# An encoder front's query and key buffer given back after the scores, with vector work placed between its matrix pieces

## The chip, the cores and the metric

The kernel runs on one core of a Trainium2 chip. The metric is the time of one execution in microseconds on the device. Five engines work side by side, each through its own instructions in order: TensorE (PE, with its weight loads shown apart as PEld), VectorE (DVE), ScalarE (ACT), GpSimd (POOL) and SyncE (SP). SP issues most transfers, POOL the gathers and scatters by index. An instruction that waits holds up everything behind it on its engine.

## What is computed

Two layers with residuals on x of shape (4, 1024, 256), in float32:

```python
x = x + attn(layernorm(x))     # causal attention, 16 heads of 16, slopes on the positions, over the 1024 tokens
x = x + ffn(layernorm(x))
# ffn, on its input z:
#   q, k, v = z @ in_proj_w.T     attention among the 4 batch entries of one token (4 x 4 scores, 16 heads)
#   h = layernorm(z + ctx @ out_w.T)
#   top two experts of 8 by h @ router_w.T; assign = the larger index of the two
#   out = layernorm(h + w2[assign](gelu(w1[assign](h))))
```

The second attention is small: for each token, the four batch entries look at each other. It needs no TensorE for scores and sums; VectorE multiplies and adds. The experts then need tokens sorted by expert, so they start from tables of which token goes where.

## The kernel before, in words

**Causal attention.** It is cut into 20 units: 12 of 256 queries (three chunks of four batch entries), then 8 of 128 queries. Each unit has four groups of heads, and each group some rounds. TensorE makes scores (tiles `sk`), ScalarE the exponentials (`p`), TensorE the weighted sums (`pv`). The rounds run in a fixed order, two per place: the loop at L2273 calls `score_next`, then `E_slot` (vector work), `D_slot` (matrix work of others), then `score_next`, `weigh_next` and `E_slot` again. So work of other parts enters TensorE's queue only at these places, between the two scores of a place.

**Encoder fronts.** `front(i, ...)` (L1573) does the second layer up to the router for block i, i = 0 to 7, 128 tokens of each of the four batch entries. It is a generator. At each yield it names the kind and the planned cost of its next piece: "E" and "P" vector work, "N" ScalarE, "R" a root on POOL, "D" matrix work, "d" matrix work that follows at once, "DQ" matrix work that needs the buffer `qkv`. The order in one front: statistics and norm into `u`; turn `u` into `ut` (D); add a bias row to x and store it (E); project to queries, keys, values and router columns, one batch entry t at a time (DQ, d, d, d); four score pieces, each a product `pr` and its sum over heads into `sc`; softmax of `sc`; four pieces of weighted values (`pv`, then sums into `ctx`); turn `ctx` (D); output projection `ao` added to `u` (D, d); norm, router key, the token's expert (`expert`, `hot`), its scaling and store; its place among the tokens of its expert (D). The last front (i = 7, `last=True`) makes the value half of the projection inside the score pieces and sums the weighted values on TensorE (`turned_sum`, L1694).

**The buffer.** Queries, keys, values and router columns of a front lie in one tile, `qkv`, 128 x 4 x 776 numbers, of which there is one. `held["qkv",]` is set when a front's DQ piece is issued (L2111 in the loop, L2366 in the tail) and removed at L1721, after the last weighted value. While it is set no other front issues its DQ. `pr` and `pv` share the tag "pr", with two buffers.

**Who comes when.** `running` holds at most two fronts; a front is queued when the last of its four units is added into x (`projected`, L2164) and starts when there is a place (`start_fronts`, L2070). `take_E` (L2076) goes over the running fronts and issues their vector pieces that are ready by the planner's own clock, as long as the planned VectorE is at most `AHEAD` = 1 us past the planned TensorE. `take_D` (L2100) issues matrix pieces up to a planned `D_SLOT` = 10 us per place, all pieces of one front as far as they go, then the other's; the planned costs are 2.8 for DQ and 2.6 for each d, so three of the four fit into one place. When front 5 is placed, `tabulate_first` (L1283) is put at the head of `running`: it makes the table of the tokens of blocks 0 to 5, 18 expert tiles of 128 tokens.

**The tail.** After the last weighted sum (L2290) what is left of the units is flushed: `invert`, `load_y`, `divide` (due_E) and `project` (due_D) of unit 18; the last unit is then normalised on TensorE and VectorE (`normalise(2)`, `normalise(3)`, L1135) and projected (`project_slots`, L1144), which completes x for front 7. Four calls of `experts.fetch` follow, each of which gathers a tile and loads its weights if a table is there; then `load_layer` loads the other weights. The loop at L2389 takes pieces of front 7, of whatever fronts still run, and of `prepare_rest`, by planned time, and puts steps of expert tiles (`tile_step`, L2381) where TensorE would be free before the next piece. It holds back the last 5 of the 18 tiles (`HELD_BACK`) until front 7's tokens are counted (`count_all`, L1257). `tabulate_rest` then makes the second table, and the other tiles run: 38 in all.

Of the kernel before, what the change touches and what calls it, by code (L numbers as in the profile page):

```python
# [29 lines left out]
F32 = mybir.dt.float32  # L30
# [3 lines left out]
ALU = mybir.AluOpType  # L34
# [3 lines left out]
P = 128  # L38
B, T, C = 4, 1024, 256
H, D, E = 16, 16, 8  # L40
S = 32
G = H // 4
NT = T // P
CC = C // P
QC = 512
# [560 lines left out]
def fast_layer(ctx: ExitStack, tc: tile.TileContext, odd, x, wq, wk, wv, wp, w_in, w_out, w_r,  # L606
# [26 lines left out]
    nc = Core(tc.nc, told)  # L633
# [92 lines left out]
    def wide(a):  # L726
        return a.unsqueeze(1).to_broadcast([P, B] + list(a.shape)[1:])
# [4 lines left out]
    at_row = con(Q_ROW)  # L732
    number_i = const("number_i", [P, 1], I32)
    nc.gpsimd.iota(number_i, pattern=[[0, 1]], base=0, channel_multiplier=1)
    pos = fact.tile([P, T], F32, tag="pr", name="pos", bufs=2)
    nc.gpsimd.iota(
        pos, pattern=[[1, T]], base=-T // 2, channel_multiplier=0,
        allow_small_or_imprecise_dtypes=True,
# [113 lines left out]
    held = {}  # L852
# [614 lines left out]
    def prepare_biases(stage):  # L1467

        if stage == 0:
            b1_rows = fact.tile([E, C], F32, tag="equal", name="b1_rows")
            nc.scalar.dma_start(
                b1_rows.rearrange("e (c p) -> e c p", p=P),
                b1.rearrange("p (e c) -> e c p", c=CC),
            )
            b2_rows = fact.tile([E, C], F32, tag="before", name="b2_rows")
            nc.scalar.dma_start(b2_rows, b2)
            b_row = fact.tile([1, 2 * C], F32, tag="u", name="b_row", bufs=2)
            for k, at in enumerate((B_IN, B_OUT)):  # L1480
                nc.scalar.dma_start(
                    b_row[:, k * C:(k + 1) * C], rows[at:at + C].unsqueeze(0)
                )
            held["biases"] = (
                (b1_rows, b_bf[0]), (b2_rows, b_bf[1]),
                (b_row[:, :C], in_bf), (b_row[:, C:], out_bf),
            )
            return
        src, three = held["biases"][stage - 1]
        if three is out_bf:  # L1490
            nc.vector.tensor_tensor(src, src, router["passed"][0:1, :C], ALU.add)
        n, width = src.shape
        rest = fact.tile([n, width], F32, tag="pr", name="rest", bufs=2)
        nc.vector.tensor_copy(rest, src)
        pieces = fact.tile([n, 3, width], BF16, tag="turned", name="pieces", bufs=TURNED)
        for k in range(3):
            nc.vector.tensor_copy(pieces[:, k], rest)
            nc.sync.dma_start(three[k * n:(k + 1) * n, :width], pieces[:, k])
            if k < 2:
                nc.vector.tensor_tensor(rest, rest, pieces[:, k], ALU.subtract)  # L1500
# [72 lines left out]
    def front(i, fact, more, last):  # L1573
# [43 lines left out]
            for_later(t)  # L1617
        store(("x", i), store_later)
        yield "DQ" if more else "D", 2.8
        qkv = fact.tile([P, B, 3 * C + E], F32, tag="qkv", name=f"qkv_{i}")  # L1620

        def projected_qkv(t, lo, hi):
            pq = bank(f"qkvp_{i}_{t}")[:, :hi - lo]
            for cc in range(CC):
                nc.tensor.matmul(
                    pq, ut[:, cc, t * P:(t + 1) * P], w_in_sb[:, cc, lo:hi],
                    start=cc == 0, stop=cc == CC - 1,
                )
                if not lo + cc:
                    nc.tensor.matmul(pq[:, :C], ones_bf, in_bf, start=False, stop=False)  # L1630
            if lo and not last:
                nc.vector.tensor_copy(qkv[:, t, lo:hi], pq)
            else:
                nc.scalar.copy(qkv[:, t, lo:hi], pq)

        for t in range(B):
            projected_qkv(t, 0, QC)
# [4 lines left out]

        def routed():
            nc.vector.tensor_tensor(
                u_[:, :, C:], qkv[:, :, 3 * C:], wide(router["b_out"]), ALU.add
            )

        if not last:
# [4 lines left out]
        for t in range(B):  # L1653
            yield "E", 2.4, 0.9 if last else 0.0
            if last:
                projected_qkv(t, QC, 3 * C + E)
            pr = fact.tile([P, B, C], F32, tag="pr", name=f"pr_{i}_{t}", bufs=2)
            nc.vector.tensor_tensor(pr, wide(qkv[:, t, 0:C]), qkv[:, :, C:2 * C], ALU.mult)
            nc.vector.tensor_reduce(
                sc[:, t], pr.rearrange("p s (h d) -> p s h d", d=D), AX.X, ALU.add  # L1660
            )
        yield "E", 1.1
        over_s = lambda a: a.rearrange("p t s h -> p t h s")
        top = small.tile([P, B, H], F32, tag="top", name=f"top_{i}", bufs=1)
# [11 lines left out]
        nc.vector.tensor_tensor(sc, sc, each_s(tot), ALU.mult)  # L1676

        def weighted(t):
            pr = fact.tile([P, B, C], F32, tag="pr", name=f"pv_{i}_{t}", bufs=2)
            nc.vector.tensor_tensor(  # L1680
                pr.rearrange("p s (h d) -> p s h d", d=D),
                qkv[:, :, 2 * C:3 * C].rearrange("p s (h d) -> p s h d", d=D),
                sc[:, t].unsqueeze(3).to_broadcast([P, B, H, D]),
                ALU.mult,
            )
            return pr
# [26 lines left out]
        else:  # L1713
            ctx_ = fact.tile([P, B, C], F32, tag="ctx", name=f"ctx_{i}")
            for t in range(B):
# [1 line left out]
                pr = weighted(t)  # L1717
                nc.vector.tensor_tensor(pr[:, 0:2], pr[:, 0:2], pr[:, 2:4], ALU.add)
                nc.vector.tensor_tensor(ctx_[:, t], pr[:, 0], pr[:, 1], ALU.add)
        if more:  # L1720
            held.pop(("qkv",))  # L1721
        if not last:
            if i < PC * (NC - 2):
                yield "N", 0
# [337 lines left out]
    def product(cost, what):  # L2062
        taken.clear()
        what()
        end = on_tensor(cost)
        busy("DVE", OF_D * cost, end - 0.5 * cost)
        read_at(max(end + READ, time["DVE"]))
        return end
# [7 lines left out]
    def take_E(some=True):  # L2076

        start_fronts()
        left = some
        while left:  # L2080
            left = False
            for it in list(running):
                now, kind = time["PE"], it.kind
                if kind not in ("E", "N", "R", "P"):
                    continue
                on = {"E": "DVE", "P": "DVE", "N": "ACT"}.get(kind)
                if it.ready > max(now, time[on] if on else 0.0) + EARLY_BY:
                    continue
                if on == "DVE" and time["DVE"] > now + AHEAD:
                    continue  # L2090
                if kind == "R":
                    it.ready = max(now, it.ready) + ROOT
                else:
                    it.ready = busy(on, it.cost if on == "DVE" else 0.5, it.ready)
                left = True
                it.next()
                if it.kind == "end":
                    running.remove(it)

    def take_D(cost):  # L2100

        for it in list(running):
            while it.kind[0] in "Dd":
                if it.kind == "DQ" and ("qkv",) in held:
                    break
                if it.kind != "d" and it.ready > time["PE"] + EARLY_BY:
                    break
                if cost and cost + it.cost > D_SLOT:
                    break
                if it.kind == "DQ":  # L2110
                    held["qkv",] = True  # L2111
                cost += it.cost
                end = product(it.cost, it.next)
                it.ready = max(end + READ, time["DVE"])
            if it.kind == "end":
                running.remove(it)

    begins = [0]
# [52 lines left out]
    def pop_due(due, now):  # L2171
        some = sorted((it for it in due if it[0] <= now), key=lambda it: it[0])
        for it in some:
            due.remove(it)
        return [(cost, what) for _, cost, what in some]
# [52 lines left out]
            experts.fetch()  # L2228
        take_E(some)

    def D_slot(p):
        todo = of_D.pop(p, []) + pop_due(due_D, time["PE"])
        for cost, what in todo:
            product(cost, what)
        take_D(sum(cost for cost, _ in todo))

    for p in range(-6, 0):
        E_slot(2 * p)
# [34 lines left out]
    for p in range(len(rounds) // 2):  # L2273
        then = p < len(rounds) // 2 - 1
        score_next(2 * p)
        E_slot(2 * p)
        D_slot(p)
        fill()
        take_E(then)
        score_next(2 * p + 1)  # L2280
        if len(waiting) > 2:
            weigh_next(waiting[:2])
            del waiting[:2]
        fill()
        E_slot(2 * p + 1, then)
# [5 lines left out]


    assert not of_E and not of_D, (sorted(of_E), sorted(of_D))
    for _, what in pop_due(due_E + [], 1e9) + pop_due(due_D + [], 1e9):
        what()
    for it in running:
        it.ready = 0.0
    for g in range(2, G):
        normalise(g)
    load_sums(last_unit)  # L2300
    project_slots()
    tail = ctx.enter_context(pool("tail", 1))
# [205 lines left out]
```

## Time and profile before

| what | us |
|---|---|
| time, median of 3 runs (lowest to highest) | 827.07 (824.54 to 828.95) |
| the profiled execution: its own time | 827.67 |
| the profiled execution: span of its instructions | 825.9 |
| busy: PE, PEld, DVE, ACT, POOL | 708.6, 532.4, 544.8, 416.5, 253.6 |
| last weighted sum of the causal attention begins | 617.66 |
| x complete for front 7 (`x<-x,op`) begins | 632.57 |
| first expert tile on PE (`mtp`) | 667.26 |
| `counts_all` of front 7's experts on PE | 723.86 |

All rows but the first are of one profiled execution. Times in the trace count from its span's start. Its own time is 1.8 us longer than its span. The program's helper for issuing is line 587, so most instructions carry L587 and have to be told apart by their tiles. A row of the time line reads: start, duration, engine, line, operation, out<-in, shape, count, and in brackets how long the engine had been idle and what ended that. One name can stand for a neighbour, since two products share a pair of PSUM banks: `qkv<-op` or `qkv<-qkp` is the copy of `qkvp` too.

### The profile page before, as it was taken

The numbers are of one execution on the slowest core, as the hardware profiler recorded it, in microseconds if no ns is written. First come the engines' busy times: TensorE is split into PE (matmuls) and PEld (weight loads), VectorE is DVE, ScalarE is ACT, GpSimd is POOL, SyncE is SP. The second block draws the span as 40 slices with busy tenths as digits, with TensorE's granted clock in tenths as the row PEclk, the third lists the DMA queues.
The fourth block names the chain that finished last, engine by engine and source line by source line (L and its number), as shares of the span: only waits on it lengthen the run. The fifth ranks groups of instructions, "written<-read, shape, count | busy, mean of one in ns | idle before, by whom it ended". The sixth has DMA issues, their size and how long they took to land. (4 is left out here: it accounts for less than half of the span.)

```text
span 825.9 us, 22497 instructions
## 1 busy us (share of the span) xinstructions
PE 708.6 (86%) x8917; PEld 532.4 (64%) x8917; DVE 544.8 (66%) x1316; ACT 416.5 (50%) x625; POOL 253.6 (31%) x360
## 2 busy tenths in 40 slices
PE   3988878999999999998998998999983689677882
PEld 2766656667666656565787876788662368566771
DVE  7335403739489768847966648497684779885663
ACT  1554535647547656635665757487550236233540
POOL 5533211313021222111222211122120235638885
PEclk9899898999999999999999999999995699988996
DMA  7444444435234234423554556255125512234430
GB/s 218 120 149 147 115 126 139 137 98 169 82 105 136 91 97 127 131 74 98 140 157 118 163 162 158 57 156 166 36 75 198 178 47 89 89 96 127 128 97 25
DMA packets 75220, 99.57 MB, mean 121 GB/s; under 512 B 19496, under 2 KB 58723, under 8 KB 74596
## 3 DMA queue, kind: packets, MB, share of 16 engines
q1 hardware_dynamic: 62272, 67.84, 28.3%
q10 hardware_dynamic: 7972, 16.05, 6.2%
q0 software_dynamic: 4864, 14.16, 5.7%
q8 instruction: 73, 1.20, 0.7%
q14 instruction: 39, 0.32, 0.1%
HBM read 61.55 MB, written 35.12 MB: 117 GB/s over the span
## 5 line engine op out<-in xcount | busy, mean ns | idle before, releaser
L587 ACT ACTIVATE p<-sk 128x1024 f32<-128x1024 f32 (+1 forms) x320 | 287.8, 939 | 160.6 <-PE sk L587 139.4
L1005 POOL TENSOR_SCALAR_AFFINE_SELECT p<-p 128x512 f32<-128x512 f32 (+1 forms) x160 | 105.6, 664 | 396.6 <-ACT p L587 394.6
L587 PE MATMUL sk<-slots 32*128 32x128 f32 (+1 forms) x3456 | 181.1, 328 | 21.5 <-DVE kq L587 8.4
L587 PEld LDWEIGHTS sk<-slots 32*128 32x128 f32 x3456 | 137.2, 187 | 65.0 <-issue 24.8
L587 PE MATMUL pv<-p,v 128*32 128x128 f32 (+1 forms) x3456 | 143.4, 312 | 9.9 <-DVE count L587 2.9
L587 PEld LDWEIGHTS pv<-p,v 128*32 128x32 f32 x3456 | 95.9, 110 | 46.9 <-issue 7.8
L587 PE MATMUL qkvp<-w_in,ut 128*128 128x264 f32 (+1 forms) x228 | 80.3, 488 | 0.0
L587 PEld LDWEIGHTS qkvp<-w_in,ut 128*128 128x128 f32 x228 | 40.8, 193 | 26.9 <-issue 22.4
L587 PE MATMUL oe<-w,ge 128*128 (+1 forms) x152 | 43.4, 410 | 14.4 <-DVE given L587 6.0
L587 PE MATMUL qkp<-xt,wqk 128*128 128x256 f32 x224 | 55.5, 392 | 0.2 <-ACT p L587 0.2
L1839 POOL DMA_INDIRECT given<-rows,rows x38 | 43.5, 1144 | 27.4 <-DVE at_t L587 11.4
L587 DVE COPY qkv<-qkvp 128x264 f32<-128x264 f32 x28 | 12.1, 432 | 54.1 <-PE qkvp L587 54.1
L587 PEld LDWEIGHTS qkp<-xt,wqk 128*128 128x128 f32 x224 | 40.9, 191 | 10.5 <-issue 3.3
L587 PE MATMUL hid<-mt,w 128*128 128x128 f32 x304 | 47.2, 293 | 0.4 <-ACT ge L587 0.4
L587 ACT COPY qkv<-qkvp 128x512 f32<-128x512 f32 (+1 forms) x29 | 16.1, 557 | 59.0 <-PE qkvp L587 47.1
L587 PEld LDWEIGHTS hid<-mt,w 128*128 128x128 f32 x304 | 42.2, 201 | 1.9 <-ACT ge L587 0.9
L1955 POOL DMA_INDIRECT out_dram<-o,out_rows x38 | 38.9, 1024 | 8.7 <-issue 5.9
L587 DVE TENSOR_TENSOR pv<-qkv,sc 128x1024 f32<-128x1024 f32 x32 | 40.2, 1257 | 0.6 <-PE ctp L587 0.6
L587 DVE TENSOR_REDUCE sc<-pr 128x64 f32<-128x1024 f32 x32 | 39.0, 1220 | 1.1
L587 DVE TENSOR_TENSOR pr<-qkv 128x1024 f32<-128x1024 f32 x32 | 39.6, 1238 | 0.0
L587 PEld LDWEIGHTS oe<-w,ge 128*128 128x128 f32 x152 | 27.2, 200 | 19.1 <-DVE given L587 7.4
L587 PE MATMUL vp<-wv,xt 128*128 128x256 f32 x128 | 34.4, 414 | 0.0
(316 smaller groups left out, 1017.9 us busy)
## 6 DMA issues: line engine op xcount, KB each, us to landing
slots<-k SPq DMA_DIRECT2D x128, 80.0 KB
k<-kq SPq DMA_DIRECT2D x32, 256.0 KB
v<-v ACTq DMA_DIRECT2D x4, 1152.0 KB
x<-in_x_dram SPq DMA_DIRECT2D x16, 256.0 KB
y<-yt SPq DMA_DIRECT2D x16, 256.0 KB
rows<-x SPq DMA_DIRECT2D x32, 128.0 KB
slots<-k SPq DMA_DIRECT2D x64, 64.0 KB
rows<-u SPq DMA_DIRECT2D x8, 512.0 KB
```

Source lines behind the costliest of these rows:

```text
L587: ins = made(*args, **kwargs)
L1005: nc.gpsimd.affine_select(blocks, blocks, pattern=[[0, 2], [0, size], [1, P]], compare_op=ALU.is_ge, fill=0.0, base=0, channel_multiplier=-1,)
L1839: nc.gpsimd.indirect_dma_start(out=self.hx, out_offset=None, in_=t.rows_of, in_offset=bass.IndirectOffsetOnAxis(ap=t.rows_[:, self.j:self. ...
L1955: ins = nc.gpsimd.indirect_dma_start(out=out.rearrange("t n c -> (t n) c"), out_offset=bass.IndirectOffsetOnAxis(ap=t.table.out_rows[:, t. ...
```

## The change

The buffer `qkv` becomes two: `qk` (queries and keys, 128 x 4 x 512, one buffer, still tagged "qkv") and `vr` (values and router columns, 128 x 4 x 264, two buffers). `held` is removed after the last score piece. The scratch `pr` has one buffer instead of two; in the last front every second weighted value uses the buffer of `ctx`. In the planner, `take_D` calls `take_E` after each matrix piece, so that vector pieces are issued between the matrix pieces of one place; at the last place of the attention it doesn't (`some` is false). After the attention, the last unit's `normalise(2)` and `normalise(3)` are issued before unit 18's `project`.

```diff
-        qkv = fact.tile([P, B, 3 * C + E], F32, tag="qkv", name=f"qkv_{i}")
+        qk = fact.tile([P, B, QC], F32, tag="qkv", name=f"qkv_{i}")
+        vr = fact.tile([P, B, C + E], F32, tag="vr", name=f"vr_{i}", bufs=2)
...
-            if lo and not last:
-                nc.vector.tensor_copy(qkv[:, t, lo:hi], pq)
+            if not lo:
+                nc.scalar.copy(qk[:, t], pq)
+            elif last:
+                nc.scalar.copy(vr[:, t], pq)
             else:
-                nc.scalar.copy(qkv[:, t, lo:hi], pq)
+                nc.vector.tensor_copy(vr[:, t], pq)
...
-            pr = fact.tile([P, B, C], F32, tag="pr", name=f"pr_{i}_{t}", bufs=2)
-            nc.vector.tensor_tensor(pr, wide(qkv[:, t, 0:C]), qkv[:, :, C:2 * C], ALU.mult)
+            pr = fact.tile([P, B, C], F32, tag="pr", name=f"pr_{i}_{t}")
+            nc.vector.tensor_tensor(pr, wide(qk[:, t, 0:C]), qk[:, :, C:], ALU.mult)
             nc.vector.tensor_reduce(
                 sc[:, t], pr.rearrange("p s (h d) -> p s h d", d=D), AX.X, ALU.add
             )
+
+        if more:
+            held.pop(("qkv",))
         yield "E", 1.1
...
         def weighted(t):
-            pr = fact.tile([P, B, C], F32, tag="pr", name=f"pv_{i}_{t}", bufs=2)
+            pr = fact.tile(
+                [P, B, C], F32, tag="ctx" if last and t % 2 else "pr", name=f"pv_{i}_{t}"
+            )
...
-        if more:
-            held.pop(("qkv",))
...
-    def take_D(cost):
+    def take_D(cost, some):
...
                 end = product(it.cost, it.next)
+
                 it.ready = max(end + READ, time["DVE"])
-            if it.kind == "end":
+                take_E(some)
+            if it.kind == "end" and it in running:
                 running.remove(it)
...
-    for _, what in pop_due(due_E + [], 1e9) + pop_due(due_D + [], 1e9):
+    for _, what in pop_due(due_E + [], 1e9):
+        what()
+    for g in range(2, G):
+        normalise(g)
+    for _, what in pop_due(due_D + [], 1e9):
         what()
     for it in running:
         it.ready = 0.0
-    for g in range(2, G):
-        normalise(g)
```

The two other tiles tagged "pr" (positions at the start, the remainder of the bias split) lose their second buffer as well, and the readers of `qkv` read `qk` or `vr`.

More of the change, by code (lines that the diff above doesn't have):

```diff
@@ L734, in fast_layer @@
     nc.gpsimd.iota(number_i, pattern=[[0, 1]], base=0, channel_multiplier=1)
-    pos = fact.tile([P, T], F32, tag="pr", name="pos", bufs=2)
+    pos = fact.tile([P, T], F32, tag="pr", name="pos")
     nc.gpsimd.iota(
@@ L1492, in prepare_biases @@
         n, width = src.shape
-        rest = fact.tile([n, width], F32, tag="pr", name="rest", bufs=2)
+        rest = fact.tile([n, width], F32, tag="pr", name="rest")
         nc.vector.tensor_copy(rest, src)
@@ L1644, in routed @@
             nc.vector.tensor_tensor(
-                u_[:, :, C:], qkv[:, :, 3 * C:], wide(router["b_out"]), ALU.add
+                u_[:, :, C:], vr[:, :, C:], wide(router["b_out"]), ALU.add
             )
@@ L1678, in weighted @@
         def weighted(t):
-            pr = fact.tile([P, B, C], F32, tag="pr", name=f"pv_{i}_{t}", bufs=2)
+            pr = fact.tile(
+                [P, B, C], F32, tag="ctx" if last and t % 2 else "pr", name=f"pv_{i}_{t}"
+            )
             nc.vector.tensor_tensor(
                 pr.rearrange("p s (h d) -> p s h d", d=D),
-                qkv[:, :, 2 * C:3 * C].rearrange("p s (h d) -> p s h d", d=D),
+                vr[:, :, 0:C].rearrange("p s (h d) -> p s h d", d=D),
                 sc[:, t].unsqueeze(3).to_broadcast([P, B, H, D]),
@@ L2229, in E_slot, with D_slot @@
         take_E(some)
-    def D_slot(p):
+    def D_slot(p, some=True):
         todo = of_D.pop(p, []) + pop_due(due_D, time["PE"])
@@ L2234, in D_slot @@
             product(cost, what)
-        take_D(sum(cost for cost, _ in todo))
+        take_D(sum(cost for cost, _ in todo), some)
     for p in range(-6, 0):
@@ L2276, in fast_layer @@
         E_slot(2 * p)
-        D_slot(p)
+        D_slot(p, then)
         fill()
```

## The prediction

> **What bounds the kernel now.** I read the busy times by stage first, cutting at the events of the table above: x of blocks 4 and 5 complete at 445, the causal attention's end at 620, the first expert tile at 667, the count of the last front's experts at 724. The columns are the stretch, its length, busy time and instructions of PE, PEld, DVE, ACT and POOL, the granted clock, the DMA share and GB/s.
>
> ```profile
> 445.00:620.00 175.00, 164.17 (x3416) 130.71 (x3406) 123.42 (x270) 110.58 (x148) 37.89 (x60) 1.00 0.43 121
> 620.00:667.00 47.00, 26.51 (x107) 16.35 (x100) 28.44 (x74) 6.76 (x13) 5.49 (x5) 0.69 0.49 165
> 667.00:724.00 57.00, 45.61 (x301) 39.40 (x301) 51.20 (x135) 25.95 (x56) 32.34 (x33) 0.94 0.29 85
> 724.00:826.00 102.00, 71.79 (x505) 62.34 (x502) 63.01 (x195) 34.00 (x75) 69.13 (x99) 0.88 0.30 94
> ```
>
> Up to 620 PE sets the pace (164 of 175 us) and DVE has about 50 us free. From 620 to 667 nothing is full: that is a chain. From 667 to 724 DVE is nearly full (51 of 57). After 724 the remaining tiles follow each other at about 3.1 us each (their turns on PE, `mtp`, go from 744.08 for the 19th to 803.81 for the 38th: 59.7 / 19).
>
> Then I read the time line for the fronts, and the waits for what held them.
>
> ```profile
> 547.44 0.41 DVE L587 TENSOR_TENSOR x<-x,op 128x256 f32<-128x256 f32 x1
> 563.07 0.18 DVE L587 TENSOR_TENSOR rank<-place,hot 128x32 f32<-128x32 f32 x1
> 566.39 0.42 DVE L587 BATCH_NORM_STATS2 stats_u<-x 128x6 f32<-128x256 f32 x1
> ...
> 645.49 1.29 POOL L1839 DMA_INDIRECT given<-rows,rows  x1 [6.82 <-DVE out_f L587]
> 655.51 1.07 ACT L587 COPY qkv<-qkvp 128x512 f32<-128x512 f32 x2 [11.81 <-DVE pv L587]
> ```
>
> x of block 6 is complete at 547.4, but its front starts at 566.4, only after front 4 has placed its tokens (563.1) and left the list of two. At the attention's end front 6 has made just its scores (the last ends at 616.3) and front 5 was placed only at 607.8, so the first table is made inside the tail, and the first gather waits for it until 645.5. Front 7 has its turned input at 643.7, but its query copies stand 11.8 us until the last read of `qkv` by front 6.
>
> **The buffer.** Each odd front waits in this way for the even one of its pair. Front 5: its projection begins at 510.5, beside front 4's last weighted value (511.2); front 4's scores ended at 499.5. Front 3: 347.0, after 343.2; front 2's scores ended at 327.1. Front 1: 208.5, beside 209.8; front 0's ended at 191.8. So about 11 to 20 us per pair, less what the places allow: they lie 5 to 14 us apart and take 10 planned us each. I take 10 to 15 us for a pair.
>
> These add up by the list of two. Front 1 is placed at 311.3 and front 3's statistics begin at 314.0, though its x was complete at 266.2; so front 3 gains front 1's 10 to 15 us and its own. It is placed at 457.0 now, and fronts 4 and 5 have been queued since 444.0, their statistics at 454.7 and 457.6. With front 3 gone before 444 they begin about 10 us sooner. Front 4 then frees its place 10 to 20 us sooner, and front 6 starts up to 19 us sooner (547.4 instead of 566.4). Front 5 gains the 10 and its own 15 to 20: placed about 580 instead of 607.8. The first table needs some 15 us of places after that (counts, three vector pieces, the product `who_first`), so I expect it made by about 600 to 615, before the attention ends. That is the step on which most hangs.
>
> **Vector work between matrix pieces.** No instruction is added; they change order. In a place with DQ, d, d PE works 8.2 us (296.4 to 304.6) and DVE only copies 0.43 us of every 2.72; the other front's 2.4 us pieces now fit between. A copy may come up to 2.4 us later, but a piece uses one pair of banks and there are four.
>
> **Scratch single.** Product and reduction are on one engine, and the 64 such instructions have 1.1 us of idle time before them in all:
>
> ```profile
> 601.79 1.22 DVE L587 TENSOR_TENSOR pr<-qkv 128x1024 f32<-128x1024 f32 x1
> 603.05 1.22 DVE L587 TENSOR_REDUCE sc<-pr 128x64 f32<-128x1024 f32 x1
> 604.18 1.22 DVE L587 TENSOR_TENSOR pr<-qkv 128x1024 f32<-128x1024 f32 x1
> ```
>
> DVE is busy throughout, so a second buffer overlaps nothing here: cost 0. Only in front 7 does PE read the scratch; there the two tags alternate as the two buffers did. If that cover fails, each of four pieces waits for its `ctp`, 1.1 us, as one did (0.56 us at 707.5): at most 4 us. The Trainium skill, "Trainium Kernel Development and Optimization", Best Practices, asks for double buffers; it means transfers beside compute, and by it the sum would be -20 less a loss that the page doesn't price, by the row it stays -20.
>
> **The wait that is added.** The next front's first query copy on ACT can now stand behind the last score piece on DVE (2.4 us and up to 1 us of planned lead). Exponentials queue behind it on ACT, and then scores on PE. It takes the place of the wait for weighted values, which cost 2.3 us at 211.1. Three pairs: 0 to 3 x 1 us; I take 0.
>
> **The sum, from the profiled span of 825.9 us.**
> 1. Attention's end: matrix work of front 6 and the table comes in ahead of 620: `ctp` 1.1, four `ao` 4.1, `who_first` 1.3, so +6; some of PE's 11 us of gaps fill. I take +5 (0 to +7).
> 2. From there to x: `yn` (628.71 to 631.2, 2.5 us) moves ahead of unit 18's product and lies beside it: -2.
> 3. From x to front 7's statistics (633.0 to 635.1) DVE does table and softmax, which would be past: -2.
> 4. Front 7's queries: 643.98 to 665.1 for four products and copies. Three products ran in 4.9 us, so four with their copies need 7: -14. The first score piece then also escapes front 6's `u` sums (665.6 to 667.0): -1.
> 5. In 667 to 724 DVE is the limit, and front 6's rows there (norm, key, rank, scaling) sum to 10.3 us: -10 if front 6 is through by then (0 if not).
> 6. Against that: 13 tiles must be done before the count at 723.9, as now. They need 13 x 2.74 = 36 us of PE (681.24 to 683.98 for one), front 7 about 19 (turn 1.0, queries and keys 5.2, values 4.2, sums 4.2, output 4.0), together 55, in a stretch that would shrink to about 60. With the table ready they can start at about 632 instead of 667, if the weights are there: the layer weights, issued from 624.5, had landed by 636 (6 GB/s from there, 371 just before). But the last tiles will be late: +4 (0 to +10).
>
> Sum: 5 - 2 - 2 - 15 - 10 + 4 = -20. The span becomes 806, the time 807.67 from the profiled 827.67; the median shown lies 0.6 us lower, so **807 us**. With the best ends of 1, 5, 6 (0, -10, 0) it is -29 and 798; with 7 us of tail filled by idle PE besides, 791. With the worst (+7, 0, +10) it is -2, which is rival two.
>
> A further row on the tail: after PE's 5.8 us wait for `yc` the clock granted in 626 to 632 was half.
>
> ```profile
> 626.00:632.00 6.00, 5.80 (x16) 4.75 (x16) 2.87 (x6) 0.00 (x0) 0.00 (x0) 0.50 0.96 352
> ```
>
> The four `wp_slots` products and the unit's projection ran there. The Trainium skill, "TensorE: Matmul & The Clock Gate", Part 1: The HAM clock gate, says that an idle window of some 3.4 us halves the clock. By it a front 7 that follows tiles without such a gap makes its four products in 5.2 us rather than 6.5, and the sum would be -21 rather than -20.
>
> **Rivals.**
> One: the table is still late. If front 5 gains less than about 10 us of its 28, the tail keeps its table, gathers at 645, and front 6's rows. Then only steps 2 and 4 count, and step 4 shrinks, since DVE was full from 632 to 656 (22.3 of 24): -10, 817 us. For it: D slots are capped at 10 planned us, and a fourth piece always goes to the next place. Against it: DVE and PE both have room in 445 to 620.
>
> Two: the tiles give it back. A shorter chain leaves fewer gaps for tiles, and every one left over costs 3.1 us after the count. With 6 of the 13 left over: -20 + 6 x 3.1 = about -1, 826 us. For it: the stage before 724 is already 80% PE and 90% DVE. Against it: 47 us between 620 and 667 in which PE has 20 idle and no tile at all runs.
>
> Three, slower: DVE gets in PE's way. Where two fronts overlap DVE is full, and PE waits for its copies: in 250 to 275 DVE was busy 24.1 of 25 us and PE 22.7, against PE's mean of 23.8 between 175 and 600. If the denser order makes all 17 such stretches like that, PE's idle time goes from 19.6 to 17 x 2.3 = 38 us: +19. It decides once the tail gains less than that, above all with rival one's -10: +9, 836 us. For it: every vector piece is now pulled ahead of copies that free banks. Against it: the planner's limit of 1 us of lead stays.
>
> That the change doesn't do what it says would show as odd fronts starting where they do now; the 11.8 us wait says that the buffer binds, and I count this in rival one.
>
> **How the numbers follow.** Forecast 0.54 (807), rival one 0.19 (817), rival two 0.12 (826), rival three 0.15 (836). About 0.5% (4.1 us) is what a measurement of this kernel can tell from no change. Faster by more: 0.54 + 0.19 = 0.73; within: 0.12; slower: 0.15. The range goes from the best ends of the sum, 791, through rivals one and two, to 829; it leaves out rival three and a little at the low side.
>
> **What would show it.** Right: front 5's `rank<-place` before 590; `given` gathers before 632; front 6's statistics near 548; no ACT wait above 4 us at `qk`; `mtp` before 640; `counts_all` near 700; about 13 tiles ahead of it. Wrong: the first gather after 640 (rival one), under 10 tiles before the count (rival two), the last weighted sum after 630 with more PE idle time before it (rival three).

## The result, and the profile after

The changed kernel takes 830.42 us (median of 13 runs, 827.72 to 834.92), the kernel before beside it 827.65 us (13 runs, 824.54 to 830.17). The ratio is 1.004, with a 95% interval of 1.0017 to 1.0063: slightly slower, where 807 us was forecast. The profiled execution of the changed kernel took 827.75 us, 0.03 us above the lowest of its 13, so its trace explains where a gain of 20 us went, but not the last 3 us of the median.

Busy time by stage, after, with the columns of the prediction's first table:

```profile
445.00:620.00 175.00, 163.02 (x3294) 129.01 (x3287) 117.94 (x265) 107.98 (x145) 35.77 (x57) 0.98 0.43 123
620.00:667.00 47.00, 35.13 (x281) 26.05 (x275) 26.00 (x57) 13.83 (x28) 15.09 (x14) 0.89 0.59 199
667.00:724.00 57.00, 37.80 (x219) 32.71 (x218) 48.69 (x128) 20.89 (x44) 22.62 (x26) 0.80 0.20 61
724.00:826.00 102.00, 73.89 (x505) 63.48 (x504) 63.95 (x197) 33.45 (x75) 69.24 (x99) 0.88 0.30 92
```

The cuts are those of before: the attention's last weighted sum now ends at 623.6 instead of 620.4, the first tile comes at 638.6, and the count (724.5) and the end stand where they did. Tiles have moved from the third stage into the second (PE 26.5 to 35.1 us there, 45.6 to 37.8 in the third), but the count comes no sooner: it isn't tiles that fill the third. VectorE still has 48.7 of 57 us.

The last unit of block 6 (unit 15), before:

```profile
521.83 0.56 SPq L1067 DMA_DIRECT2D sums<-y  x1
...
541.18 0.43 DVE L587 TENSOR_TENSOR yc<-yc,su 128x256 f32<-128x256 f32 x1
...
544.14 1.13 PE L587 MATMUL op<-wp,yc 128*128 128x256 f32 x4
```

The time line of block 6, after:

```profile
533.24 0.56 SPq L1067 DMA_DIRECT2D sums<-y  x1
...
546.25 0.18 DVE L587 TENSOR_TENSOR rank<-place,hot 128x32 f32<-128x32 f32 x1
...
553.86 0.54 DVE L587 TENSOR_TENSOR yc<-yc,su 128x256 f32<-128x256 f32 x1 [4.03 <-DMA slots<-k]
554.41 1.16 PE L587 MATMUL ao<-w_out,ct 128*128 128x264 f32 x4
...
557.52 1.05 PE L587 MATMUL ao<-w_out,ct 128*128 128x264 f32 x4
...
562.71 1.13 PE L587 MATMUL op<-wp,yc 128*128 128x256 f32 x4
563.88 0.42 DVE L587 TENSOR_TENSOR x<-x,op 128x256 f32<-128x256 f32 x1 [1.98 <-PE op L587]
566.47 0.42 DVE L587 TENSOR_SCALAR rstd_u<-mv_u 128x4 f32<-128x4 f32 x1
```

Front 4 leaves its place at 546.3 instead of 563.1. But x of block 6 (unit 15's projection added) is now complete at 563.9 instead of 547.4, so front 6's statistics end at 566.5, only 2 us sooner than before (568.6). Of the 16.4 us, 11.4 lie ahead of the load of unit 15's sums (`sums<-y`, 533.24 instead of 521.83), and 5.9 between its division and its projection (3.0 us before, 8.85 now), where front 5's four `ao` went first; the pieces between and behind them give 0.9 back.

The SP queue around unit 17, before (SPq is the time an issue takes there):

```profile
585.30 0.60 SPq L1090 DMA_DIRECT2D su<-r  x1
...
596.66 3.61 SPq L1129 DMA_DIRECT2D wp_slots<-in_wp_dram  x8
```

The same after, and behind it SP's wait for the memset (us in total, times, longest):

```profile
584.00 0.35 SPq L1075 DMA_DIRECT2D r<-inverse  x1
...
597.25 0.99 POOL L1127 MEMSET wp_slots<- 128x512 f32 x2
...
597.80 2.22 SPq L1129 DMA_DIRECT2D wp_slots<-in_wp_dram  x5
...
601.46 0.61 SPq L1090 DMA_DIRECT2D su<-r  x1
...
605.95 0.42 DVE L587 TENSOR_TENSOR yc<-yc,su 128x256 f32<-128x256 f32 x1 [10.51 <-DMA yc<-y]
606.60 3.64 PE L587 MATMUL pv<-p,v 128*32 128x128 f32 x64 [4.27 <-issue]
```

```profile
SPq L1129 <- POOL wp_slots L1127: 12.9, 1, 12.9
```

Unit 17's inverse is stored at 584.4, but its loads `su` and `yc` go out only at 601.5: ahead of them in SP's order stand the loads of `wp_slots`, which wait for a memset on POOL at 597.25. VectorE stands 10.5 us before the division and TensorE 4.3 us, and then its weighted sums take 3.64 us. (The profile names nothing that TensorE waited for; its idling ends 0.2 us after the division, and e4 below doesn't have it.) The granted clock of that stretch:

```profile
606.00:611.00 5.00, 4.40 (x80) 4.05 (x84) 4.62 (x18) 1.29 (x2) 0.99 (x1) 0.50 0.28 86
```

The Trainium skill, "TensorE: Matmul & The Clock Gate", Part 1, has the array fall to half clock after an idle window of about 3.4 us. The trace agrees roughly: in these 4.27 us of idling the clock fell to 0.50 at 605.2, after 2.9 us. In the kernel before the loads stood the other way round (`su` at 585.30, `wp_slots` at 596.66) and VectorE did not wait.

The tail, after:

```profile
623.33 1.29 POOL L1845 DMA_INDIRECT given<-rows,rows  x1 [0.79 <-issue]
638.59 0.63 PE L587 MATMUL mtp<-ident,given 128*128 128x128 f32 x2
646.18 0.77 PE L587 MATMUL utp<-ident,u 128*128 128x128 f32 x3
647.11 0.76 PE L587 MATMUL utp<-ident,u 128*128 128x128 f32 x5 [0.16 <-ACT u L587]
653.18 1.02 PE L587 MATMUL qkvp<-w_in,ut 128*128 128x512 f32 x2
666.08 1.22 DVE L587 TENSOR_TENSOR pr<-qkv 128x1024 f32<-128x1024 f32 x1
697.65 2.08 PE L587 MATMUL ctp<-ident,pv 128*128 128x128 f32 x8 [6.50 <-DVE pv L587]
699.54 0.19 DVE L587 TENSOR_TENSOR hot<-low_con,expert 128x32 bf16<-128x32 f32 x1
724.46 0.24 PE L587 MATMUL counts_all<-hot,ones_bf 128*128 128x8 bf16 x4 [7.18 <-DVE hot L587]
```

Gathers begin at 623.3 instead of 645.5, tiles at 638.6 instead of 667.3. Front 7's x is complete at 638.83 (632.57 before), its first score begins at 666.1, as before (666.9), and the count is at 724.5, as before. Front 6's experts are known at 699.5, 16 us later than before (683.1).

In the table times count from the end of the first front's statistics, since that point itself moves by up to 5 us between executions (147.6 to 152.7). Each column is one trace, and rows of the same program differ too: x of block 6 comes at 396.1 to 399.4 in three traces whose program is that of the kernel before up to there (before, e3, e11), and at 416.2 to 423.7 in eight with that of the changed kernel, but for the place of one load (after, e4 to e10). So a shift of 3 us in an upper row says little; one counts that lies clear of such a range. e4 and e13 are explained below.

| us | before | after | e4 | e13 |
|---|---|---|---|---|
| x of block 6 complete | 399.4 | 416.2 | 416.7 | 406.1 |
| front 6's statistics end | 420.6 | 418.8 | 419.3 | 409.9 |
| front 5 placed | 459.8 | 432.4 | 431.0 | 434.7 |
| front 6's softmax begins (`top`) | 486.1 | 491.5 | 481.4 | 454.8 |
| front 6's experts known (`hot`) | 535.1 | 551.9 | 541.8 | 510.2 |
| x complete for front 7 | 484.5 | 491.2 | 481.1 | 484.8 |
| from there to its first score | 34.3 | 27.2 | 27.2 | 25.5 |
| from there to the count | 91.3 | 85.6 | 85.0 | 75.0 |
| from the count to the last scatter's end | 94.9 | 94.5 | 94.7 | 94.4 |

### The profile page after: what moved, and what is told of

Read it like the earlier page. It is cut to its first block, busy times and chain, and to the rows that moved or that the text cites. A ratio compares the mean times of both kernels' runs of the same rounds, so it can differ in the third digit from the quotient of the medians.

```text
span 826.1 us, 22490 instructions
## 1 busy us (share of the span) xinstructions
PE 713.5 (86%) x8917; PEld 538.1 (65%) x8917; DVE 543.3 (66%) x1316; ACT 416.1 (50%) x625; POOL 250.7 (30%) x360
## 5 line engine op out<-in xcount | busy, mean ns | idle before, releaser
L1005 POOL TENSOR_SCALAR_AFFINE_SELECT p<-p 128x512 f32<-128x512 f32 (+1 forms) x160 | 101.6, 638 | 433.9 <-ACT p L587 431.9
L587 PEld LDWEIGHTS pv<-p,v 128*32 128x32 f32 x3456 | 97.2, 111 | 49.3 <-issue 11.4
L587 PE MATMUL qkvp<-w_in,ut 128*128 128x264 f32 (+1 forms) x216 | 72.4, 471 | 0.0
L587 PEld LDWEIGHTS qkvp<-w_in,ut 128*128 128x128 f32 x216 | 38.6, 190 | 25.4 <-issue 21.0
L587 PEld LDWEIGHTS qkp<-xt,wqk 128*128 128x128 f32 x224 | 40.9, 191 | 10.6 <-issue 3.6
L587 DVE TENSOR_TENSOR pv<-vr,sc 128x1024 f32<-128x1024 f32 x32 | 39.3, 1228 | 0.3
L587 DVE COPY vr<-qkvp 128x264 f32<-128x264 f32 x28 | 12.1, 432 | 38.4 <-PE qkvp L587 38.3
L587 ACT COPY qkv<-qkvp 128x512 f32<-128x512 f32 x22 | 12.9, 586 | 43.9 <-PE qkvp L587 43.9
```

The source lines that it names most:

```text
L587: ins = made(*args, **kwargs)
L1005: nc.gpsimd.affine_select(blocks, blocks, pattern=[[0, 2], [0, size], [1, P]], compare_op=ALU.is_ge, fill=0.0, base=0, channel_multiplier=-1,)
```

## The experiments

Each ratio is to runs of the kernel before on the same chip (their medians lay between 827.15 and 828.79 us). The text in each quotation was on record before the run.

**The parts alone.** e1 has the buffers only: no `take_E` in `take_D`, and the last unit's `normalise` behind unit 18's product as before.

> The buffers of the change alone (queries and keys given back after the scores, values in two, scratch single); no vector work between matrix pieces, unit 18's product before the normalising as before. Theory A (PE is full until 620, so what is pulled ahead pushes the causal units back; front 6 can't start sooner, and the tail's chain is set by fronts 6 and 7 on DVE): front 5 is placed about 590 to 600 instead of 607.8, x of block 6 is complete 5 to 10 us later than 547.4, and the time is within 4 us of before. Rival B (the buffers gain, and the vector work between matrix pieces loses it again by coming ahead of copies PE waits for): 10 to 20 us faster than before.

Measured: 836.42 us, ratio 1.0106 (1.0068 to 1.0144). Neither theory foresaw that: x of block 6 is complete 17 us later (564.65) instead of 5 to 10, front 5 is placed at 601.3, and the time is about 9 us longer. e2 has the other planner edit only, in the kernel before:

```diff
+                take_E(some)
```

> The vector work between matrix pieces alone; one buffer held until the last weighted value, as before. Theory A: odd fronts start their projection as late as before, the time is within 4 us of before. Rival B: PE waits more for copies between 175 and 600 (idle above the 19.6 us of before by 10 us or more), and the time is 10 us or more above before.

Measured: 832.15 us, ratio 1.0072 (1.0043 to 1.0101): slower than theory A allowed by a little, and without rival B's idle time on TensorE (below). e3 has the kernel before with only `normalise(2)` and `normalise(3)` moved.

> Only the two normalisings of the last unit ahead of unit 18's product. My step 2 said -2 us, and it should be seen alone: x for front 7 complete about 630.6 instead of 632.6, the time 0 to 2 us lower. If the order of DVE's work there doesn't matter, because the product of the last unit then runs in a row at half clock, the time is the same within 1 us.

Measured: 826.08 us, ratio 0.9991 (0.9964 to 1.0018), which allows either expectation; the last two additions into x lie 2.0 us apart instead of 4.2.

The buffers alone have the highest ratio, though e1's interval and e2's overlap. In e1 x of block 6 comes at 415.3, as late as after, and in e2 and e3 (old buffer) at 399.2 and 396.1: so the buffers are what delays it. Between the split alone (1.0106) and the whole change (1.004) the vector work between pieces and the moved `normalise` together gain about 5 us, though the first of the two in the kernel before costs 6. So rival three (VectorE in TensorE's way) isn't the cause: TensorE's idle time in 175 to 600 is 19.6 us before, 19.2 after, 18.8 in e2, and higher only in e1 (22.5). Why e2 loses 0.7% is not settled: its x for front 7 comes 3.3 us later, after a wait for `yc` of 9.05 us instead of 6.71, and such rows move by as much without a change.

**The stuck load.** e4 issues the slots' weights two units sooner.

```diff
-    at_E(2 * begins[last_unit] + 1, load_slotted)
+    at_E(2 * begins[last_unit - 2] + 1, load_slotted)
```

> The changed kernel, with the loads of the last unit's projection weights issued two units earlier. In the changed kernel unit 17's loads of y stand on SP behind these weights (they are issued at 601.5, 17 us after the inverse at 584.0; before it was 2.9 us), DVE waits 10.5 us for them and PE 4.3 us, then runs at half clock. Theory A with this as the added cost: the y loads come at about 587, DVE's wait of 10.5 us is gone, the attention ends about 5 us sooner, and the time is 4 to 6 us below the changed kernel. Rival: the wait is covered by what PE had to do anyway, and the time is within 1 us of the changed kernel.

Measured: 823.83 us, ratio 0.9937 (0.9904 to 0.9969), about 8 us under the changed kernel by the ratios, more than the 4 to 6 expected. There is no wait for unit 17's `yc`, and x for front 7 comes 10 us sooner (481.1 instead of 491.2; in e5 to e10 between 481.5 and 488.9). But the stall has only moved. In e4's time line, behind unit 15's inverse at 541.74:

```profile
545.65 0.98 POOL L1127 MEMSET wp_slots<- 128x512 f32 x2
546.20 2.67 SPq L1129 DMA_DIRECT2D wp_slots<-in_wp_dram  x6
...
551.14 1.31 SPq L1129 DMA_DIRECT2D wp_slots<-in_wp_dram  x2
552.49 0.60 SPq L1090 DMA_DIRECT2D su<-r  x1
```

Unit 15's `su` now goes out 10.8 us after its inverse, at a place where x of block 6 waits for it.

**What sets the stage before the count.** Four kernels on top of e4. e5 holds back 2 instead of 5 tiles (`HELD_BACK`).

> The changed kernel with the earlier weight loads (e4), and 2 of the first 18 tiles held back instead of 5. In the changed kernel 13 tiles are through by 693 and PE then stands nearly idle until the count at 724. Theory A (the tail's chain is DVE's work of fronts 6 and 7 and of the tiles; tiles given out ahead of the count cost DVE 1.75 us each and save 3.1 us each behind it): 16 tiles ahead of the count, the time 2 to 6 us below e4. Rival (tiles give it back, as rival two of the prediction: the stage after the count isn't shortened by the tiles done, or the chain grows as much): within 2 us of e4.

Measured: 816.58 us, ratio 0.989 (0.9849 to 0.993), which overlaps e4's. 16 tiles are ahead of a count 86.4 us after x (85.0 in e4), and the last stage is 88.2 us instead of 94.7: TensorE had room (busy 31.4 of the last 51 us before e4's count).

e6 leaves out the four `experts.fetch` calls right after the attention.

> e4 without the four fetches right after the attention: gathers and own weights are issued by the tail's steps instead. In e4 the last unit's y arrives 4.9 us after its issue (before: 2.5 us) while five gathers run, and PE idles 7.0 us. Theory C (the early gathers and loads delay y): DVE's wait for y falls from 9.5 to about 7 us, x for front 7 is complete 2 to 3 us sooner, but the first tile comes later; the time is between 2 us less and 4 us more than e4. Theory that early tiles are worth little, since 13 are done long ahead of the count: the time is within 2 us of e4.

Measured: 822.40 us, ratio 0.9958 (0.9932 to 0.9984), as e4. The wait for the last `yc` falls from 9.51 to 7.80 us, the first tile comes at 639.2 instead of 632.7, and x for front 7 no sooner (481.5 beside 481.1), against theory C. So tiles that start sooner gain nothing here, where 13 of them are through long before the count.

e7 gives the scaling of `u` in fronts 6 and 7 to POOL.

> e4 with the two scalings of u in fronts 6 and 7 (2.5 us of DVE each) on POOL. Theory A (DVE sets the chain from x to the count): the count and the end come 2 to 5 us sooner than in e4. Rival (the chain is latency between engines, or POOL's own queue of gathers suffers): within 2 us, or slower.

Measured: 828.55 us, ratio 1.003 (1.0004 to 1.0055), about 8 us worse than e4 by the ratios. The time line of e7:

```profile
687.46 3.17 DVE L587 TENSOR_TENSOR key<-key,best 128x32 f32<-128x32 f32 x1
688.23 2.34 POOL L1799 TENSOR_TENSOR u<-u,rows 128x1024 f32<-128x1024 f32 x1
690.65 2.34 POOL L1800 TENSOR_TENSOR u<-u,rows 128x1024 f32<-128x1024 f32 x1
690.66 2.36 DVE L587 TENSOR_SCALAR key<-key 128x32 f32<-128x32 f32 x1
```

Tiny VectorE operations that took 0.19 and 0.18 us in e4 last as long as POOL's: nothing was taken off VectorE. So e7 doesn't tell what less vector work is worth.

e8 does: front 6's four weighted values, about 9 us of VectorE, are left out (one copy stands in, so front 6's second attention isn't computed).

> e4, but front 6 leaves out its four weighted values: their place is taken by one copy of its values, so 8.2 us of DVE work leave the tail, and the output differs. It measures step 5 of the prediction (what it is worth that front 6's work is out of the tail). Theory A: 6 to 9 us below e4. If DVE isn't what the chain waits for: less than 3 us below e4.

Measured: 823.98 us, ratio 0.9946 (0.9922 to 0.997), as e4. From x to the first score it is 27.2 us in both. In e8's time line VectorE waits for TensorE in the time set free:

```profile
647.50 0.43 DVE L587 BATCH_NORM_STATS2 stats_v<-oe 128x6 f32<-128x256 f32 x1 [3.18 <-PE oe L587]
...
654.77 0.69 DVE L587 COPY ct<-ctp 128x512 f32<-128x512 f32 x1 [5.88 <-PE ctp L587]
```

My theory that VectorE's load sets that stretch fell with this run.

e9 tests TensorE's written order: from the turn of front 7's input until its eight projections are issued, no tile and no matrix piece of front 6 goes to TensorE.

```diff
+        if 3 <= asked[0] <= 8 and it is not last_front and it.kind[0] in "Dd":
+            return 1e9
...
             tile_begin() + TILE_HALF < at and experts.waiting() > HELD_BACK
+            and not 3 <= asked[0] <= 8
```

> The kernel of e4 (slots' weights loaded early), but from the turn of front 7's input until its eight projections are issued, no expert tile and no matrix piece of front 6 is put on TensorE. In e4 front 7's first score product begins 27.2 us after its x is complete, with VectorE idle for some 6.8 us between 650.8 and 660.1, while expert tiles 3 to 5 and front 6's turn and output projection stand between its queries on TensorE; from 660.1 to 702.5 VectorE has no gap. Theory P (the written order on TensorE sets the first score, and VectorE's work from there to the last weighted value): first score 17 to 19 us after x, the count 5 to 8 us sooner than e4's 717.8, 13 tiles still ahead of it, time 4 to 7 us below e4 (817 to 820). Theory T (the tiles give it back): the tiles that moved back are late, 12 or fewer are through before the count or TensorE is full there, and the time is within 2 us of e4 (822 to 826). Theory V (VectorE's total work alone, wherever its gaps lie): the first score moves, but the gap opens elsewhere, and the count stays within 2 us of 717.8.

Measured: 821.57 us, ratio 0.9891 (0.9852 to 0.9931). Time line of e9:

```profile
645.78 2.81 PE L587 MATMUL utp<-ident,u 128*128 128x128 f32 x8 [2.68 <-ACT u L587]
648.41 2.08 PE L587 MATMUL qkvp<-w_in,ut 128*128 128x512 f32 x2
...
659.37 1.22 DVE L587 TENSOR_TENSOR pr<-qkv 128x1024 f32<-128x1024 f32 x1
```

The queries follow the turn at once (7 us after it in the changed kernel), the first score begins 20.4 us after x instead of 27.2, and the count comes 79.6 us after it instead of 85.0. That is theory P, with the first score 1 to 3 us later than it said: TensorE ran at half clock there (two products in 2.08 us instead of 1.02). In the time the gain is about 4 us by the ratios, but the two intervals overlap, so the count shows it and the time only suggests it.

The clock in e9:

```profile
641.00:642.00 1.00, 0.88 (x8) 0.87 (x9) 0.97 (x4) 0.46 (x3) 0.00 (x0) 0.98 1.04 410
642.00:648.00 6.00, 3.27 (x14) 2.02 (x13) 5.69 (x15) 3.95 (x7) 3.62 (x4) 0.50 1.01 380
```

It fell to 0.50 at 642.0, ahead of the 2.68 us of idling and just behind one of 1.95 us (639.2 to 641.1). That is shorter than the window that the page above gives; what else made it fall, no run here tells.

e10 is e9 with 2 tiles held back, e11 the kernel before with 2 held back.

> e9 with 2 instead of 5 of the first 18 tiles held back until the count, as in e5 (816.6, 16 tiles before the count at 716.0). Theory P: the count 4 to 8 us before e5's, 16 tiles ahead of it if TensorE has room, time 810 to 814. Theory T: TensorE has no room for three more tiles in a shorter stretch; the count comes no sooner than in e5 and the time is 815 to 819.

Measured: 815.93 us, ratio 0.9846 (0.9824 to 0.9868). The count is 6.2 us later after x than in e9 (85.8) and the last stage 8.8 us shorter. That is theory T: with three more tiles ahead of it the count comes hardly sooner than in e5 (86.4).

> The kernel before with one number changed, 2 instead of 5 tiles held back. If the room for more tiles ahead of the count comes from the change (first table made 45 us sooner), 16 tiles can't all be done before a count at 724: the time stays within 2 us of the kernel before, or gets worse by what the tiles add to the chain. If the room was there anyway (13 tiles were ahead of the count in both kernels), the time falls by as much as from e4 to e5, 5 to 9 us, and nothing of e5's gain is the change's.

Measured: 824.70 us, ratio 0.9961 (0.9943 to 0.9978). The count comes 5 us later after x than in the kernel before (96.3), the last stage is 7.5 us shorter. From e4 to e5 the ratio fell by 0.0047, here by 0.0039: this gain isn't the change's. It was smaller than expected.

**Who pushes block 6 back.** e12 is e4 with smaller places for the fronts' matrix work in units 13 to 15.

```diff
-                if cost and cost + it.cost > D_SLOT:
+                if cost and cost + it.cost > most:
...
-        take_D(sum(cost for cost, _ in todo), some)
+        few = begins[13] <= p < begins[16]
+        take_D(sum(cost for cost, _ in todo), some, 6.0 if few else D_SLOT)
```

> The kernel of e4 with at most 6 instead of 10 planned microseconds of the fronts' matrix work in each place of units 13 to 15, so that two pieces instead of three go into a place. It tests whether the work of fronts 4 and 5, pulled forward by the split buffer, is what pushes the last unit of block 6 back. Counted from the end of the first front's statistics, x of block 6 is complete after 399.4 us in the kernel before and after 416.7 in e4. Theory Z (TensorE is full in 445 to 620, so what one stream gains the other loses): x of block 6 comes 5 to 12 us sooner than in e4 (405 to 412) and front 5 is placed 8 us or more later than e4's 431.0 from the same point; the time stays within 4 us of e4 or gets longer by up to 6, 822 to 830. Rival (unit 15 is late for another reason, such as its transfers): x of block 6 moves by less than 3 us.

Measured: 816.35 us, ratio 0.985 (0.9818 to 0.9882). x of block 6 comes at 409.1 instead of 416.7, front 5 is placed at 438.2 instead of 431.0: what one stream gains the other loses, as theory Z said (7.2 us, where it said 8 or more). Its time was wrong: front 5's delay shows no cost (the first gather is at 621.2, in e4 at 619.6), and front 6 has its softmax and half of its weighted values behind it before the tail.

e13 has the same edit in the changed kernel, without e4's; e14 in the kernel before.

> The changed kernel with e12's edit alone (at most 6 planned microseconds of the fronts' matrix work in the places of units 13 to 15), the slots' weights loaded where the change has them. If the two causes stand side by side: x of block 6 from the first statistics 5 to 10 us sooner than the changed kernel's 416.2, front 6's softmax before the end of the attention, its expert known (hot) by about 670 instead of 699.5, and the time 5 to 9 us below the changed kernel, 821 to 826 beside a kernel before of 828; the load of unit 17's sums still stands behind the slots' weights. If e12's gain needs e4's order of loads, the time stays at 828 to 832.

Measured: 811.17 us (808.80 to 812.72), ratio 0.9802 (0.9777 to 0.9827), the fastest of all. Time line of e13:

```profile
555.78 0.42 DVE L587 TENSOR_TENSOR x<-x,op 128x256 f32<-128x256 f32 x1 [0.15 <-PE op L587]
...
559.52 0.17 DVE L587 TENSOR_SCALAR rstd_u<-mv_u 128x4 f32<-128x4 f32 x1
...
592.82 0.61 SPq L1090 DMA_DIRECT2D su<-r  x1
...
600.24 0.99 POOL L1127 MEMSET wp_slots<- 128x512 f32 x2
...
604.38 0.58 DVE L587 TENSOR_REDUCE top<-sc 128x64 f32<-128x256 f32 x1
...
659.80 0.19 DVE L587 TENSOR_TENSOR hot<-low_con,expert 128x32 bf16<-128x32 f32 x1
...
709.41 0.24 PE L587 MATMUL counts_all<-hot,ones_bf 128*128 128x8 bf16 x4
```

Front 6's softmax is inside the attention (604.4), its experts are known at 659.8, the count comes 75.0 us after x. The stage from 667 to the count is 42 us instead of 57, with 37.4 of VectorE in it instead of 48.7:

```profile
667.00:709.00 42.00, 35.72 (x225) 30.33 (x224) 37.42 (x101) 19.32 (x42) 24.11 (x27) 0.96 0.23 67
```

And unit 17's loads now stand ahead of the slots' weights (592.8 against 600.2), so the stuck load is gone with no edit to it. I had expected it to stay, and 821 to 826 us. I take it that the two causes are not two, and both hang on how far the planner has shifted the units; no run separates them further. That e12 is slower than e13 (the intervals just overlap) may come from e4's edit, which in e12 too holds unit 15's `su` for 11 us after its inverse (540.84 to 551.80); in e13 it is 3.1.

> The kernel before with the same edit. If fewer pieces in units 13 to 15 pay by themselves, the time falls here as it did from e4 to e12, by 5 us or more. If they pay only where the split buffer has pulled fronts 4 and 5 forward (theory Z), they put work off here that nothing makes up: front 5 is placed later than 607.8, the table later, and the time is the same or up to 6 us longer, 827 to 834.

Measured: 826.20 us, ratio 0.998 (0.9949 to 1.0011), the same; x of block 6 (398.4) and front 5's placing (458.4) hardly move. So the smaller places are worth nothing by themselves, and 2.4% in the changed kernel (from 1.004 to 0.9802).

e15 is e12 with 2 tiles held back.

> e12 with 2 instead of 5 of the first 18 tiles held back until the count, as in e5 and e10. In e12 13 tiles are ahead of a count 74.7 us after x is complete, and TensorE is busy 40 of the last 45 us before it. If there is room for three more (some 8 us of TensorE): 16 tiles ahead, the count 0 to 5 us later than in e12, the last stage 6 to 7 us shorter, and the time 809 to 815. If not: the count is later by the 8 us, and the time stays at 815 to 819.

Measured: 816.74 us, ratio 0.9874 (0.9846 to 0.9901): nothing gained over e12. The count is 8.3 us later after x (83.0), the last stage 7.8 us shorter. TensorE was busy 40 of the 45 us before e12's count, against 31.4 of 51 in e4, so the three tiles pushed the count back by what they saved behind it.

## Why the prediction was wrong

**The buffer: the first half right.** Front 3 was placed 13 us sooner, front 5 at 580.0 where I had said about 580, the first table's product at 597.6 (600 to 615), the gathers at 623.3 (before 632), and no query copy waited over 4 us on ScalarE. Rival one (table late) is out.

**The step that failed** is "Front 4 then frees its place 10 to 20 us sooner, and front 6 starts up to 19 us sooner (547.4 instead of 566.4)". The place was free at 546.3, as said. But 547.4 is the end of unit 15 in the old order, and I kept it fixed while pulling two fronts' matrix work ahead of it on an engine that my own first table shows busy 164 of 175 us. I counted what comes in ahead of 620 (+5 us at the attention's end) and not what goes behind it. e1 has the same delay with the split alone; e12 and e13 take work out of the way and x of block 6 comes back, by 7.6 and 10.1 us. Both lie clear of the eight traces above, and e15, the same program as e12 up to there, has 409.1 again. So that much of the 16.8 us is shown; 6.7 us are left in e13, and whether they too are displaced work stays open.

**Terms 3 and 5** (-2 and -10) hung on this step, and gave nothing: front 6's softmax went from 486.1 to 491.5 instead of into the attention, its experts from 535.1 to 551.9. In e13, where front 6 does start sooner (10.7 us, counted from the first statistics), x to the count falls by 16.3 us from the kernel before, against 5.7 in the change. So the two terms, 12 us together, nearly hold where their condition does (10.6 us more), and in the change the condition failed.

**Term 4** (-15) was mis-sized. The wait for the buffer is gone, but from x to the first score only 7.1 us went. I let four products run in 7 us behind the turn and put the rest of the 21 us down to the buffer. But in the kernel before, too, front 6's turn and output projection stand between these products (`ctp` from 648.7 to 658.0, `ao` at 660.5 and 664.4), and they stayed. After, the planner put two tiles between the turn and the first product, and then front 6's turn and output projection between the others: 653.2 to 664.3 for the queries with their copies. e9 takes that away and gives 6.9 us. A freed wait of one stream on an engine with a written order is filled with others' work, which is then ahead of it.

**Terms 1 and 2** had nothing for SP's queue. The attention's last weighted sum ended about 3 us later, inside 0 to +7, but for another reason in part: 4.3 us of TensorE's idling and 1.7 us at half clock behind the stuck load. The moved `normalise` did bring the last two additions together (4.2 to 3.1 us; 2.0 in e3), while the wait for `yc` grew from 6.7 to 10.7 us, with the gathers issued beside it (7.8 in e6 without them). So x for front 7 came 6.3 us later where the sum had +3. e4 shows what the stuck load was worth: about 8 us, and it had no step in my list at all.

**Term 6** (+4) didn't occur: the count-to-end stage is as long as before (94.5 and 94.9). Rival two (tiles give it back) is wrong for the change, and right in e15, where the stage has become short enough.

**Scratch single: right, 0.** VectorE never idles ahead of any of the product, sum and score instructions of the fronts (156 rows of `pr`, `sc`, `pv` and `ctx` in the trace after; 0.56 us in all before). A second buffer had nothing to overlap here.

**The sum.** x for front 7: +3 forecast, +6.3 measured. x to the count: 2 + 15 + 10 = 27 us less forecast, 5.7 measured. Count to end: +4 forecast, -0.4 measured. In the profiled execution these cancel to +0.2 us. The other 2.7 us of the median are not resolved by one trace.

Open: why e2 alone loses; whether front 7's queries first (e9) adds to e13, whose first score is still 25.5 us after x. Neither was tried.

## What to carry to other kernels

When a freed buffer lets one stream go earlier on an engine that is full, ask what it displaces, and whether that is the input of the very step you hope to start sooner: here three pieces instead of two per place turned -2% into +0.4%. Reordering one engine's program also moves where other queues' instructions stand, so look for loads that wait for something (here a memset) and list what is behind them. Putting more work ahead of a serial point pays only while the engine has idle time there: with TensorE 31 of 51 us busy it gave 0.5%, with 40 of 51 (the kernel before) 0.4%, with 40 of 45 nothing.

## What the hardware showed that I had not expected

A POOL operation of two SBUF inputs stopped VectorE outright: beside POOL's 2.34 us products in e7, VectorE operations of 0.18 to 0.42 us took 2.36 to 3.17 us, four times out of four. The Trainium skill, "Trainium Architecture — The Big Picture", What this means for kernel authors, calls the shared port of the two an exclusive lock and not a split of bandwidth; e7 agrees, and shows that even a 128x32 operation is held for as long as POOL runs.
